# Channel mix in float32r over two-part coefficients, with contiguous row levels and whole column transforms

## The chip, the cores and the metric

The kernel runs on one core of one Trainium2 chip. The metric is the device time in microseconds of one execution, the median of the runs shown; a profile of one execution stands beside it. The engines are called PE (TensorE), DVE (VectorE), ACT (ScalarE), POOL (GpSimd) and SP (SyncE, which only issues transfers here).

## What is computed

The input x has the shape 4 x 64 x 256 x 256 (batch, channel, height, width), in float32. Four layers follow one another; 0, 1 and 3 are long convolutions, and layer 2 works in the Haar domain:

```python
# layers 0, 1, 3: a separable causal filter per channel, and a residual
k = einsum('ijk,imk->ijmk', hx, hy)[0]      # hx, hy: two small sine networks
y = irfft2(rfft2(x) * rfft2(k) / fft_size)[..., :L, :L]
x = y + x * bias[:, None, None]
# layer 2
f1 = haar2d(x)                               # rows and columns, 8 levels each
acc = 0
for i in range(2):
    f4 = einsum('bchw,oc->bohw', f1 * v[i], conv_w[i])
    acc = acc + sign(f4) * relu(abs(f4) - tau[i])
x = haar2d(acc, inverse=True) + x
```

## The kernel before

A convolution of layers 0, 1 and 3 is two products on PE with Toeplitz matrices, one for the columns and one for the rows; the Toeplitz tiles are read from short filters in device memory (pads) by overlapping rows. `contract` (L245) makes one such product as four matmuls in float32, two over 256 columns (L248) and two over 128 (L249).

`convolutions(b, ...)` takes one batch through layers 0 and 1 and the forward Haar transform, one channel at a time. `first` and `second` make the products a0, y0, a1, y1; ACT copies a0 and a1 from PSUM (L262), DVE adds the residual to y0 and y1 (L279). `pairs` (L312) makes the sums and differences of neighbouring columns into the tile `sd` (eight channels deep), `store` (L318) writes them to `keep` in device memory, for the end of layer 2. `levels` (L321) makes the other seven levels of the row transform for four channels at a time, in place in `sd`, with strides that double (L327 and L328, fourteen DVE instructions, of 512, 256, 128, 64, 32, 16 and 8 elements a partition, two each). The column transform inside a half of the rows is one product with a fixed matrix: `split` (L334, ACT) and `rest` (L339, DVE) cut a channel into two parts in the format float32r, and `down` (L344) adds two float32r products over 512 columns with the matrix `hbr` (L349). `down` also has a path that makes one float32 product with `hbt` (L353), which no channel takes, since `in_parts` is all channels. `away` (L358, ACT) copies the result from PSUM and SP writes it to `coef`.

`mixing(b, ...)` goes over 64 groups of four coefficient rows. `load` (L395) reads a group's coefficients of all 64 channels, two halves stacked on 128 partitions, from `coef` (SP, 3 buffers under the tag "f"). `mix` (L410) makes four float32 products a group, each with a slice of the coefficients as weights and a matrix `wb` as moving operand, 256 columns wide, which holds the mixing matrix twice with zeros between (L415). `scaled` (L432, DVE) and `scaled_too` (L436, ACT, one row of 64 elements an instruction, L439) multiply by v, then ACT takes the size and sign, DVE shrinks by tau and adds into `z`, which holds a whole batch in SBUF.

`inverse(b, ...)` takes z back, one channel at a time: `fetch` (L482) reads the kept sums and differences, `rows` (L491) makes the inverse row transform by products and transposes (L495, L496), `halves` (L501) splits the result into two float32r parts, `cols` (L507) makes the column product over 512 columns (L511), `join` (L516) adds the kept part and undoes `pairs`, and layer 3 follows. For batches 0 to 2 every third channel's layer 3 is put off: its u goes to `late` in device memory, and `convolution` (L545) takes it up beside the last mixing.

The order of the work is written out by hand. Each step is put into a list with a time in ticks (`at`, L296): the tick of its channel or group plus a fixed offset in `PLACE`. The list is sorted by this time, and the instructions are issued in that order; each engine takes its own in that order. Mixing of batch b runs beside the convolutions of batch b+1, whose 64 channels `spread` (L559) lays over the ticks up to the mixing's end; then the inverse of batch b follows with the rest of those convolutions. `border` is the tick at which a mixing ends; steps of a batch's last two groups of channels that are due after it are set three times as far apart (`after`, L304).

Of the kernel before, what the change touches and what calls it, by code (L numbers as in the profile page):

```python
# [41 lines left out]
    "away": 0.734,  # L42
    "mix load": -0.977,
# [52 lines left out]
def conv_seq_kernel(ctx, tc, x, fz, fw, bias, decay, haar, haar_row, factors, vt, taut, wmix, out):  # L96
# [33 lines left out]
    wb = const.tile([P, 2, P], F32, name="wb")  # L130
# [5 lines left out]
    sd = zpool.tile([P, 8, 2, 2, P], F32, name="sd")  # L136
    keep = [dram.tile([C, P, 2, 2, P], F32, name=f"keep{b}") for b in range(B)]
    coef = [dram.tile([2, C, P, S], F32, name=f"coef{b}") for b in range(B)]
# [67 lines left out]
    def constants():  # L206
        signs = part(P)
        nc.sync.dma_start(hbt, haar[0])
        nc.sync.dma_start(signs, haar[1])
        nc.sync.dma_start(hrow, haar_row)  # L210
        nc.vector.memset(wb, 0.0)
        for r in range(2):
            nc.sync.dma_start(wb[r * C : (r + 1) * C, r, :], wmix)
        nc.scalar.copy(hb, signs)
        nc.scalar.copy(hbr, hbt)
# [83 lines left out]
    def convolutions(b, ticks, in_parts=(), border=None):  # L299


        st = {}

# [8 lines left out]
        def pairs(c):  # L312
            v = st.pop(c)["y1"].rearrange("p k (w e) -> p k w e", e=2)
            t = sd[:, c % 8]
            nc.vector.tensor_add(t[:, :, 0, :], v[:, :, :, 0], v[:, :, :, 1])
            nc.vector.tensor_sub(t[:, :, 1, :], v[:, :, :, 0], v[:, :, :, 1])

        def store(c):  # L318
            nc.sync.dma_start(keep[b][c], sd[:, c % 8])

        def levels(steps):  # L321
            def run(n):
                t = sd[:, n % 2 * 4 : n % 2 * 4 + 4]
                for step in steps:
                    v = t[:, :, :, 0, :].rearrange("p c k (w e) -> p (c k) w e", e=2 * step)
                    even, odd = v[:, :, :, 0], v[:, :, :, step]
                    nc.vector.tensor_sub(odd, even, odd)  # L327
                    nc.vector.scalar_tensor_tensor(even, even, 2.0, odd, ALU.mult, ALU.subtract)  # L328

            return run  # L330

        parts = {}

        def split(c):  # L334

            w = parts[c] = mx.tile([P, 2, 2, S], F32R, name=f"sp_{b}_{c}", tag="sp", bufs=1)
            nc.scalar.copy(w[:, 0], sd[:, c % 8].rearrange("p k e w -> p k (e w)"))  # L337

        def rest(c):  # L339
            w = parts[c]  # L340
            t = sd[:, c % 8].rearrange("p k e w -> p k (e w)")
            nc.vector.tensor_tensor(w[:, 1], t, w[:, 0].bitcast(F32), ALU.subtract)  # L342

        def down(c):  # L344
# [7 lines left out]
            else:  # L352
                nc.tensor.matmul(  # L353
                    ps.rearrange(flat), hbt, sd[:, c % 8].rearrange("p k e w -> p (k e w)"), start=True, stop=True
# [3 lines left out]
        def away(c):  # L358
            t = io.tile([P, 2, S], F32, name=f"co_{b}_{c}", tag="co", bufs=BUFS["co"])
            nc.scalar.copy(t, parts.pop(("ps", c)))  # L360
            nc.sync.dma_start(coef[b][:, c].rearrange("k p w -> p k w"), t)
# [16 lines left out]
        for n in range(C // 4):  # L378
            end = ticks[4 * n + 3] + 4
            for s, steps in enumerate([(1,), (2, 4), (8, 16, 32, 64)]):  # L380
                at(after(end + 1 + s, n) + PLACE["levels"], levels(steps), n)
            for j in range(4):
                c = 4 * n + j
                if c in in_parts:
# [3 lines left out]
                at(after(end + 4 + j, n) + PLACE["away"], away, c)  # L388
        return after(ticks[-1] + 11, C // 4 - 1)

    def mixing(b, start, n_act):
# [3 lines left out]
        def load(g):  # L395
            f = mx.tile([P, 2, S], F32, name=f"f_{b}_{g}", tag="f", bufs=3)
            nc.sync.dma_start(f, coef[b].rearrange("k c p w -> (k c) p w")[:, 2 * g : 2 * g + 2])
# [12 lines left out]
        def mix(g):  # L410
            f = st[g]["f"]
            ps = psx.tile([P, 2, 2, S], F32, name=f"px_{b}_{g}", tag="mix")
            for q in range(2):
                for h in range(2):
                    nc.tensor.matmul(  # L415
                        ps[:, h, q, :],
                        f[:, q, h * P : (h + 1) * P],
                        wb.rearrange("p r n -> p (r n)"),
                        start=True,
                        stop=True,  # L420
                    )
# [288 lines left out]
```

## Time and profile before

| | |
|---|---|
| median of 3 runs | 2973.84 us (2973.59 to 2974.6) |
| span of the profiled execution | 2971.0 us; no other time is listed for it |
| PE busy | 2905.9 us (98%) |
| DVE busy | 2529.6 us (85%) |
| ACT busy | 2183.4 us (73%) |
| POOL busy | 0.2 us |
| transfers | 649.74 MB, mean 219 GB/s |

The span runs from the first to the last instruction of one execution. An engine is busy while one of its instructions lasts; matmul lengths are modelled and overlap, so their starts say more than their lengths. PEld is the loading of weights, which can lie beside a product. A row of a group of instructions has the line, the engine, the operation, what it writes and reads, its size and count, then the busy time in us and the mean of one in ns, then the idle time of the engine ahead of it and what ended that. A float32 product appears as two records, a float32r product as one. The columns of a table by stage are: the stage, its length, then busy time and count of PE, PEld, DVE, ACT and POOL, the clock, the busy share of the transfer engines, and GB/s.

### The profile page before, as it was taken

The page shows a single profiled execution, that of the slowest core. Times are in us where ns is not written, and L with a number is a line of the kernel's source. Part 1 is how long each engine was busy: PE and PEld are TensorE (multiplying, and loading weights), DVE is VectorE, ACT ScalarE, POOL GpSimd, SP SyncE. Part 2 cuts the span into 40 slices and gives each one's busy share as a digit, 9 for nine tenths or more (in the row PEclk, how much of TensorE's full clock was granted, in tenths as well). Part 3 has the DMA queues.
Part 4 walks back from the last instruction along what each step waited for, and adds up shares of the span by engine and source line. Part 5 has one row for each costly group of instructions (what it writes and reads, how often), then busy time and mean ns, then how long its engine had stood idle before and what let it go on. Part 6 is the DMA issues. An engine that isn't in the chain of part 4 may idle for free. (4 is left out here: it accounts for less than half of the span.)

```text
span 2971.0 us, 52173 instructions
## 1 busy us (share of the span) xinstructions
PE 2905.9 (98%) x16950; PEld 2615.2 (88%) x16950; DVE 2529.6 (85%) x4571; ACT 2183.4 (73%) x5142; POOL 0.2 (0%) x4
## 2 busy tenths in 40 slices
PE   8999999999999999999999999999999999999999
PEld 6899988888888998888888998888888998888998
DVE  5766768999988879999988878999998889998776
ACT  2333338999986768889986768999986768887554
POOL 0000000000000000000000000000000000000000
PEclk9999999999999999999999999999999999999999
DMA  5887777776667876767777876777677888777676
GB/s 156 246 235 230 225 234 213 210 208 195 210 196 238 255 222 199 210 209 208 209 220 229 255 228 199 210 211 211 206 211 231 255 245 235 234 231 220 212 211 186
DMA packets 562498, 649.74 MB, mean 219 GB/s; under 512 B 44369, under 2 KB 447412, under 8 KB 562100
## 3 DMA queue, kind: packets, MB, share of 16 engines
q1 hardware_dynamic: 482996, 562.07, 64.8%
q10 hardware_dynamic: 79232, 84.34, 8.1%
q8 instruction: 137, 2.24, 0.3%
q14 instruction: 133, 1.09, 0.1%
HBM read 426.77 MB, written 219.48 MB: 218 GB/s over the span
## 5 line engine op out<-in xcount | busy, mean ns | idle before, releaser
L248 PE MATMUL py<-t,a 128*128 128x256 f32 x3072 | 920.4, 381 | 11.7 <-ACT a L262 6.3
L262 ACT COPY a<-pa 128x512 f32<-128x512 f32 x768 | 485.8, 633 | 374.7 <-PE pa L249 338.9
L439 ACT ACTIVATE f<-px,vt 128x64 f32<-128x64 f32 x2816 | 619.9, 391 | 113.8 <-DVE f L434 113.2
L249 PEld LDWEIGHTS py<-t,a 128*128 128x128 f32 x3072 | 583.4, 190 | 79.4
L249 PE MATMUL py<-t,a 128*128 128x128 f32 x3072 | 590.0, 274 | 0.0
L248 PEld LDWEIGHTS py<-t,a 128*128 128x128 f32 x3072 | 498.4, 191 | 57.4 <-ACT a L262 18.1
L415 PE MATMUL px<-wb,f 128*128 128x256 f32 x2048 | 486.6, 380 | 6.4 <-ACT f L439 6.4
L415 PEld LDWEIGHTS px<-wb,f 128*128 128x128 f32 x2048 | 369.2, 190 | 48.3 <-ACT f L439 8.5
L248 PE MATMUL pa<-t,y 128*128 128x256 f32 x1024 | 310.0, 385 | 16.7 <-DVE y L279 15.4
L450 DVE TENSOR_TENSOR mag<-mag,vt 128x1024 f32<-128x1024 f32 x256 | 313.3, 1224 | 10.8 <-ACT mag L443 10.2
L443 ACT ACTIVATE mag<-f 128x1024 f32<-128x1024 f32 x256 | 299.8, 1171 | 20.4 <-DVE z L458 19.6
L454 DVE SCALAR_TENSOR_TENSOR mag<-mag,f 128x1024 f32<-128x1024 f32 x256 | 313.3, 1224 | 0.9
L504 ACT CAST w<-pw 128x512 fp32r<-128x512 f32 x256 | 150.3, 587 | 221.6 <-PE pw L496 208.9
L248 PE MATMUL pa<-t,x 128*128 128x256 f32 x1024 | 305.8, 380 | 1.1 <-issue 1.1
L446 ACT ACTIVATE f<-f 128x1024 f32<-128x1024 f32 x256 | 288.1, 1125 | 4.4 <-DVE y L279 1.2
L488 ACT COPY zc<-z 128x512 f32<-128x512 f32 x256 | 282.5, 1104 | 10.9 <-DVE z L289 6.3
L342 DVE TENSOR_TENSOR sp<-sd,sp 128x512 fp32r<-128x512 f32 x256 | 176.5, 689 | 105.0 <-ACT sp L337 103.6
L248 PE MATMUL pa<-t,u 128*128 128x256 f32 x772 | 231.0, 381 | 10.2 <-issue 9.5
L519 DVE SCALAR_TENSOR_TENSOR t<-r,pu 128x512 f32<-128x512 f32 x256 | 175.5, 685 | 65.6 <-PE pu L511 65.0
L279 DVE SCALAR_TENSOR_TENSOR y<-x,bsb,py 128x512 f32<-128x512 f32 x256 | 190.8, 745 | 39.3 <-PE py L249 39.2
L279 DVE SCALAR_TENSOR_TENSOR y<-y,bsb,py 128x512 f32<-128x512 f32 x256 | 190.3, 744 | 38.0 <-PE py L249 37.8
L249 PEld LDWEIGHTS pa<-t,y 128*128 128x128 f32 x1024 | 194.5, 190 | 26.4
(67 smaller groups left out, 4470.8 us busy)
## 6 DMA issues: line engine op xcount, KB each, us to landing
t<-pad SPq DMA_DIRECT2D x768, 256.0 KB, 3.9
x<-in_x SPq DMA_DIRECT2D x256, 256.0 KB, 3.6
keep<-sd SPq DMA_DIRECT2D x256, 256.0 KB, 2.9
coef<-co SPq DMA_DIRECT2D x256, 256.0 KB, 3.1
f<-coef SPq DMA_DIRECT2D x256, 256.0 KB, 3.3
r<-keep SPq DMA_DIRECT2D x256, 256.0 KB, 3.3
out_y<-y ACTq DMA_DIRECT2D x256, 256.0 KB, 4.0
late<-u ACTq DMA_DIRECT2D x63, 256.0 KB, 3.0
```

The source lines that it names most:

```text
L248: nc.tensor.matmul(ps[:, m, :], src[:, 0, m * P : (m + 1) * P], t[:, ::-1], start=True, stop=False)
L249: nc.tensor.matmul(ps[:, m, P:], src[:, 1, m * P : (m + 1) * P], t[:, : P - 1 : -1], start=False, stop=True)
L262: nc.scalar.copy(a, s["p" + new])
L279: nc.vector.scalar_tensor_tensor(y, s[res], bsb[:, layer, c : c + 1], s["p" + new], ALU.mult, ALU.add)
L342: nc.vector.tensor_tensor(w[:, 1], t, w[:, 0].bitcast(F32), ALU.subtract)
L415: nc.tensor.matmul(ps[:, h, q, :], f[:, q, h * P : (h + 1) * P], wb.rearrange("p r n -> p (r n)"), start=True, stop=True,)
L439: nc.scalar.mul(f4[:, j], px[:, j], scale(g, 0)[:, j : j + 1])
L443: nc.scalar.activation(mag, st[g]["f4"], AF.Abs)
L446: nc.scalar.activation(st[g]["f4"], st[g]["f4"], AF.Sign)
L450: nc.vector.tensor_sub(mag, mag, over(g, 1, 16))
L454: nc.vector.scalar_tensor_tensor(mag, mag, 0.0, st[g]["f4"], ALU.max, ALU.mult)
L488: nc.scalar.copy(a, z[:, :, :, c].rearrange("p h (i k) -> p h k i", k=2))
```

## The change

- The coefficients are stored in two float32r parts, high and low: `away` casts to float32r on ACT and writes the high part, a new step `low` (offset 1.05) subtracts it from PSUM on DVE and writes the rest. `coef` doubles in size; each part of a channel is written in rows of 2 KB a partition.
- `wb` holds the mixing matrix in two float32r parts. `mix` makes 16 float32r products a group, of 128 columns each: for every slice of 128 coefficient columns, one with the low and one with the high part of the matrix. High and low coefficients of the 64 channels are stacked on the 128 partitions. The group's load is 512 KB, is issued from POOL, and has 2 buffers.
- The kept sums and differences are written by two transfers, and `fetch` takes its tile from the buffers of x (tag "in").
- The row levels read and write contiguous halves, through `sums` and `less`; those of 128 and 64 stay on DVE, those of 32 to 2 are on POOL.
- `in_parts` is now filled inside `convolutions`: a channel is split only for batch 0 or where its column transform is due at or after the mixing's end; the others take the float32 product of `down`.
- Layouts of `sd`, of the inverse's tiles and of the host's tables follow; the space that POOL's transfers reserve is set to 1024.

```diff
-    wb = const.tile([P, 2, P], F32, name="wb")
+    wb = const.tile([P, 2, P], F32R, name="wb")
+    sums = zpool.tile([P, 4, 2, P], F32, name="sums")
+    less = zpool.tile([P, 4, 2, 96], F32, name="less")
-    coef = [dram.tile([2, C, P, S], F32, name=f"coef{b}") for b in range(B)]
+    coef = [dram.tile([2, C, P, 2, S], F32, name=f"coef{b}") for b in range(B)]
...
+            nc.vector.tensor_add(sums[:, c % 4], v[:, :, :, 0], v[:, :, :, 1])
+            nc.vector.tensor_sub(sd[:, c % 8, 1], v[:, :, :, 0], v[:, :, :, 1])
...
-            nc.sync.dma_start(keep[b][c], sd[:, c % 8])
+            nc.sync.dma_start(keep[b][c, :, 0], sums[:, c % 4])
+            nc.sync.dma_start(keep[b][c, :, 1], sd[:, c % 8, 1])
+        def levels(engine, lengths):
             def run(n):
-                t = sd[:, n % 2 * 4 : n % 2 * 4 + 4]
-                for step in steps:
-                    v = t[:, :, :, 0, :].rearrange("p c k (w e) -> p (c k) w e", e=2 * step)
-                    even, odd = v[:, :, :, 0], v[:, :, :, step]
-                    nc.vector.tensor_sub(odd, even, odd)
-                    nc.vector.scalar_tensor_tensor(even, even, 2.0, odd, ALU.mult, ALU.subtract)
+                t = sd[:, n % 2 * 4 : n % 2 * 4 + 4, 0]
+                for length in lengths:
+                    half = length // 2
+                    v = place(t, length).rearrange("p c k (w e) -> p c k w e", e=2)
+                    engine.tensor_tensor(place(t, half), v[..., 0], v[..., 1], ALU.add)
+                    engine.tensor_tensor(t[:, :, :, half:length], v[..., 0], v[..., 1], ALU.subtract)
+        def place(t, length):
+            if length == P:
+                return sums
+            if length == 1:
+                return t[:, :, :, :1]
+            begin = {64: 0, 32: 64, 16: 0, 8: 16, 4: 24, 2: 28}[length]
+            return less[:, :, :, begin : begin + length]
...
-            t = io.tile([P, 2, S], F32, name=f"co_{b}_{c}", tag="co", bufs=BUFS["co"])
-            nc.scalar.copy(t, parts.pop(("ps", c)))
-            nc.sync.dma_start(coef[b][:, c].rearrange("k p w -> p k w"), t)
+            t = parts["hi", c] = mx.tile([P, 2, S], F32R, name=f"hi_{b}_{c}", tag="hi")
+            nc.scalar.copy(t, parts["ps", c])
+            nc.sync.dma_start(coef[b][0, c].rearrange("p k w -> p (k w)"), t.bitcast(F32).rearrange("p k w -> p (k w)"))
+        def low(c):
+            t = mx.tile([P, 2, S], F32R, name=f"lo_{b}_{c}", tag="lo", bufs=1)
+            nc.vector.tensor_tensor(t, parts.pop(("ps", c)), parts.pop(("hi", c)).bitcast(F32), ALU.subtract)
+            nc.sync.dma_start(coef[b][1, c].rearrange("p k w -> p (k w)"), t.bitcast(F32).rearrange("p k w -> p (k w)"))
...
-            for s, steps in enumerate([(1,), (2, 4), (8, 16, 32, 64)]):
-                at(after(end + 1 + s, n) + PLACE["levels"], levels(steps), n)
+            at(after(end, n) + PLACE["levels"], levels(nc.vector, (128,)), n)
+            at(after(end + 1, n) + PLACE["levels"], levels(nc.vector, (64,)), n)
+            at(after(end + 1, n) + PLACE["levels"], levels(nc.gpsimd, (32, 16, 8, 4, 2)), n)
             for j in range(4):
                 c = 4 * n + j
-                if c in in_parts:
+                if border is None or end + 4 + j >= border:
+                    in_parts.add(c)
...
+                at(after(end + 4 + j, n) + PLACE["low"], low, c)
...
-            f = mx.tile([P, 2, S], F32, name=f"f_{b}_{g}", tag="f", bufs=3)
-            nc.sync.dma_start(f, coef[b].rearrange("k c p w -> (k c) p w")[:, 2 * g : 2 * g + 2])
+            f = mx.tile([P, 2, 2, S], F32R, name=f"f_{b}_{g}", tag="f", bufs=2)
+            nc.gpsimd.dma_start(f, coef[b].rearrange("l c p k w -> (l c) p k w")[:, 2 * g : 2 * g + 2])
...
-            for q in range(2):
-                for h in range(2):
-                    nc.tensor.matmul(
-                        ps[:, h, q, :],
-                        f[:, q, h * P : (h + 1) * P],
-                        wb.rearrange("p r n -> p (r n)"),
-                        start=True,
-                        stop=True,
-                    )
+            for h in range(2):
+                for q in range(2):
+                    for r in range(2):
+                        for i in (1, 0):
+                            nc.tensor.matmul(
+                                ps[:, h, q, r * P : (r + 1) * P],
+                                f[:, q, h, r * P : (r + 1) * P],
+                                wb[:, i],
+                                start=(i == 1),
+                                stop=(i == 0),
+                            )
...
-            r = mx.tile([P, 2, 2, P], F32, name=f"r_{b}_{c}", tag="f", bufs=3)
+            r = io.tile([P, 2, 2, P], F32, name=f"r_{b}_{c}", tag="in", bufs=3)
...
-    ready = convolutions(0, range(C), in_parts=range(C))
+    ready = convolutions(0, range(C))
...
-            ready = convolutions(b + 1, spread(ahead, end + 2), in_parts=range(C), border=end)
+            ready = convolutions(b + 1, spread(ahead, end + 2), border=end)
...
-    nc = _bacc.Bacc("TRN2", target_bir_lowering=False, num_devices=1)
+    nc = _bacc.Bacc("TRN2", target_bir_lowering=False, num_devices=1, dynamic_dma_scratch_size=1024)
```

## The prediction

> **What bounds the kernel now.** I read the page's first two parts, then each stage by windows of time, then the timeline of TensorE, because an engine that looks 98% busy may only be waiting between instructions.
>
> ```profile
> span 2971.0 us, 52173 instructions
> PE 2905.9 (98%) x16950; PEld 2615.2 (88%) x16950; DVE 2529.6 (85%) x4571; ACT 2183.4 (73%) x5142; POOL 0.2 (0%) x4
> ```
>
> Busy time per engine in the four mixing stages (from the first to the last product of L415):
>
> ```profile
> 453.00:858.00 405.00, 398.49 (x2179) 350.37 (x2179) 381.86 (x671) 396.73 (x1203) 0.00 (x0) 1.00 0.69 205
> 1088.00:1529.00 441.00, 435.14 (x2440) 391.42 (x2440) 409.39 (x717) 388.21 (x1094) 0.00 (x0) 1.00 0.71 208
> 1763.00:2203.00 440.00, 434.70 (x2436) 390.99 (x2435) 408.86 (x717) 387.70 (x1093) 0.00 (x0) 1.00 0.70 208
> 2433.00:2705.00 272.00, 266.62 (x1450) 238.83 (x1450) 265.13 (x313) 234.87 (x555) 0.00 (x0) 1.00 0.80 234
> ```
>
> TensorE idles 6 us in each of them, 23 us in all; DVE and ACT are at 88 to 98%, so they are close behind. The timeline of TensorE tells whether its busy time is real work; columns are start, length, line, records in a row:
>
> ```profile
> 1502.95 1.89 PE L415 MATMUL px<-wb,f 128*128 128x256 f32 x8
> 1504.68 0.59 PE L248 MATMUL py<-t,a 128*128 128x256 f32 x2
> 1505.11 0.38 PE L249 MATMUL py<-t,a 128*128 128x128 f32 x2
> 1505.33 0.60 PE L248 MATMUL py<-t,a 128*128 128x256 f32 x2
> ...
> 1507.08 0.38 PE L249 MATMUL pa<-t,x 128*128 128x128 f32 x2
> 1507.22 0.71 PE L349 MATMUL pz<-sp,hbr 128*128 128x512 f32 x2
> 1507.77 0.59 PE L248 MATMUL py<-t,a 128*128 128x256 f32 x2
> ```
>
> Starts, not lengths, give the cost, since lengths overlap. A float32 product is two records. The 8 records of one mixing group take 1504.68 - 1502.95 = 1.73 us (0.216 each, 256 columns); two of 128 columns take 1505.33 - 1505.11 = 0.22 us (0.11 each): the cost goes with the columns. The two float32r products of 512 columns begin after the pair at 1507.08 (0.22 us) and end at 1507.77: 0.47 us, 0.235 each. With these prices TensorE's work is 8192 x 0.216 (L248, L415) + 6144 x 0.11 (L249) + 1536 x 0.11 (L495, L496) + 1024 x 0.235 (L349, L511) = 2855 us of 2971. **The kernel is bound by TensorE's own work**, and any added product shows in the time.
>
> One more thing decides this case: what a weight load costs when no product hides it. At 113.9 us TensorE had been idle:
>
> ```profile
> 113.92 0.30 PEld L349 LDWEIGHTS pz<-sp,hbr 128*128 128x128 f32 x2 [0.80 <-issue]
> 114.26 0.19 PEld L248 LDWEIGHTS py<-t,a 128*128 128x128 f32 x1
> ```
>
> A load lasts 0.19 in the records, so the second of the pair began at 113.92 + 0.30 - 0.19 = 114.03, 0.11 us after the first. In the dense stretches each load begins as the product before it begins; so the first float32r product could start only 0.11 us after its load. The two products use the same weights (hbr) and are still loaded twice: L349 has 512 products and 512 loads.
>
> **What the Trainium skill says.** "FP8 and Floating Point Precision", TensorE Precision Notes: true FP32 takes four passes. The trace agrees: 256 columns take 2 x 0.216 us, and float32r 512 columns take 0.235 instead of four times as much. "TensorE: Matmul & The Clock Gate", LDWEIGHTS (loading the stationary operand): a load takes columns / 1.2 ns, 107 ns for 128; the trace's 0.11 agrees. The same page, Weight-path perf modes, says that the fast weight load is off for FP32 input; the 0.11 is float32r's, so it has none either. "SBUF — State Buffer", Who interferes with whom: a DVE instruction with two SBUF inputs and a GpSimd instruction that reads SBUF block each other; GpSimd does nothing in this trace, so no run here shows it.
>
> **The change part by part.**
> *Channel mix (L415).* It removes 8 records of 0.216 (1.73 us) per group and adds 16 float32r products of 128 columns, each with its own weight load, since both coefficient parts times both weight parts are summed. The trace has no float32r product of 128 columns. By its columns one takes 128/512 of 0.235 = 0.06, or 0.075 if the 0.02 that 0.235 has above 512 columns' 0.213 (twice 256 columns' single pass, 0.107) is fixed. But its load takes 0.11 and begins only as the product before starts, so 0.11 is the pace: 16 x 0.11 = 1.76 us, +0.03 us, **+8 us** for 256 groups. Bounds: 0.06 each (-197 us) and the float32 price, 0.22 (+458 us). I take 0.11, because a load is seen in the trace for every product.
> *Whole column transforms (down).* Their transforms for batches 1 to 3 that come due before the mixing's end are made in float32 in one product, without split and rest. From the ticks of spread(): 54, 53 and 53 channels; the other 10, 11 and 11 and all 64 of batch 0 stay in parts. One costs 4 passes of 512 columns = 4 x 0.216 = 0.86 us instead of 0.47: 160 x 0.39 = **+62 us**, on the bound engine. Removed beside it: 160 times ACT's split and DVE's rest, 115 and 110 us.
>
> ```profile
> L337 ACT CAST sp<-sd 128x512 fp32r<-128x512 f32 x256 | 184.0, 719 | 3.9 <-DVE sd L328 3.9
> L342 DVE TENSOR_TENSOR sp<-sd,sp 128x512 fp32r<-128x512 f32 x256 | 176.5, 689 | 105.0 <-ACT sp L337 103.6
> L505 DVE TENSOR_TENSOR w<-pw,w 128x512 fp32r<-128x512 f32 x256 | 175.3, 685 | 2.3 <-ACT w L504 2.3
> L327 DVE TENSOR_TENSOR sd<-sd 128x512 f32<-128x512 f32 x64 | 44.2, 691 | 47.9 <-DMA keep<-sd 28.2 <-DMA t<-pad 12.0 <-DMA coef<-co 2.5
> ```
>
> *low.* 256 DVE subtractions from PSUM, priced as L505: +175 us of DVE. Each waits for ACT's copy (away) and holds the bank pz about 0.3 tick longer; the fourth bank after it is wanted 0.6 tick later still, so TensorE doesn't wait. Its store waits on SP behind DVE; queued behind it are keep, x and t loads that have about a tick (6.5 us) of lead.
> *Row levels.* They are 64 x 5.15 us = 330 us on DVE (L327 and L328). Two of 512 at 0.69 and two of 256 at 0.42 (L315's price) remain, 143 us. Ten GpSimd instructions a group take the rest: 496 elements at the 4497 ns for 2048 of the page "GPSIMD Engine Reference", 3.1 Elementwise, are an estimated 1.1 us, and 0 to 0.5 us each fixed: 1 to 6 us of a group's 26. They may hold DVE as long. In the second mixing stage DVE had 409 us; with low (57 x 0.69), less levels (57 x 0.73) and rest (53 x 0.69), it has 370, and with 14 groups at 6 us 454 of some 463. So TensorE's work hides it at both ends, narrowly at the upper; past that, each us of DVE is a us of time.
> *Transfers.* coef is written and read in two parts: 2 x 256 x 256 KB = 134 MB more than 649.74. In a mixing stage that is 441 us x 208 GB/s = 92 MB plus 64 x 0.26 + 57 x 0.26 = 32 MB, so 0.71 of the engines becomes about 0.91 in a stage 22 us longer. The f loads move from SP past POOL's level instructions, with 2 buffers for 3: a load may start when the product two groups before is done, two ticks less 1.76 us before its use, 11 us (6.7 in the last mixing stage). The price from "DMA: Bandwidth & Descriptors", Anatomy of one DMA, 2.0 us + 524288/436000 = 3.2 us alone, fits; doubled by traffic it still fits, so nothing on the path, bound 0 to +64 us. SP gains 512 issues (second keep, second coef) and loses 256, at 0.33 us: 85 us of an engine that mostly waits. r moves into the buffers of x; both are live two ticks, so in the three or so ticks where a new batch's loads meet an inverse stage 4 are wanted of 3: about +3 us at each of three such places, **+9 us**. The relief of ACT and DVE may give back a third of the 23 us of idle: **-7 us**.
> Sum: 8 + 62 + 9 - 7 = **+72 us**. On the profiled span, 2971 + 72 = 3043; the median shown lies 2.8 us above this span, so 3046.
>
> **The rivals.**
> *A slower pace:* float32r in 128 columns goes at the float32 price, 0.22. For it: only 512 columns have been seen. Against it: float32 halves exactly with its columns. 2974 + 458 + 62 + 2 = 3496 us.
> *The load doesn't bind* (the side that ends faster): the loads of successive small products overlap and the pace is 0.075: 16 x 0.075 = 1.20, -0.53 us a group, -136 us; with 62 and -7, 2893 us. It decides from 1.73 - 62/256 = 1.49 us a group, 0.093 us a product. Against it: the 0.11 at 113.92.
> *Transfers bind:* at 0.91 the tiles f, x or t land late. 0.25 us a group is +64 us: 3110 us. For it: the doubled traffic and POOL's queue; against it: TensorE hardly waits at 0.80 in the last mixing stage.
>
> **How the numbers follow.** Load-bound pace 0.68, own range 3025 to 3080; transfers 0.12; slower pace 0.16; faster 0.04. The range 3015 to 3130 holds the first two, with the unknown GpSimd and transfer costs. A difference of 0.2% (6 us) is about what a measurement can tell from no change: slower 0.95, the same 0.01, faster 0.04.
>
> **What would show it.** The mix's 16 products 0.11 us apart, 1.76 us a group, with PEld near 100% there; about 160 float32 products of 512 columns, two records 0.43 apart; ACT and DVE near 80% in the mixing stages while TensorE stays at 98%. It is wrong if the 16 take 1.5 us or 3.5 us, or if TensorE waits for f.

## The result, and the profile after

The changed kernel takes 3418.53 us (median of 4 runs, 3414.4 to 3419.87) against 2974.22 us before (4 runs): 1.149 times as long, with a 95% interval of 1.147 to 1.151. The forecast was 3046 us with a range up to 3130. The direction was right, and the added time is 444 us instead of 72. The profiled execution has a span of 3418.1 us.

The first line of the page after and its line of busy times:

```profile
span 3418.1 us, 57457 instructions
PE 3123.2 (91%) x18998; PEld 2783.1 (81%) x18998; DVE 2453.4 (72%) x4027; ACT 2111.5 (62%) x4983; POOL 343.8 (10%) x900
```

No engine is as busy as the busiest was before: TensorE fell from 98% to 91%, DVE from 85 to 72%, ACT from 73 to 62%. So the question is which engine waits for which. The same four stages as before (first to last product of the mix, now L439); the columns are the stage, its length, busy time and count of PE, PEld, DVE, ACT and POOL, the clock, the transfers' share and GB/s:

```profile
457.00:987.00 530.00, 460.16 (x2686) 397.76 (x2685) 359.24 (x550) 381.58 (x1154) 79.80 (x192) 0.93 0.69 212
1217.00:1771.00 554.00, 499.11 (x2982) 437.34 (x2980) 384.96 (x595) 364.30 (x1049) 80.44 (x202) 0.96 0.74 219
2001.00:2555.00 554.00, 491.83 (x2976) 429.67 (x2974) 384.04 (x594) 363.41 (x1048) 80.48 (x202) 0.97 0.73 219
2786.00:3148.00 362.00, 302.28 (x1969) 279.12 (x1969) 278.37 (x318) 241.44 (x562) 32.82 (x62) 0.93 0.76 221
```

They have grown from 405, 441, 440 and 272 us by 125, 113, 114 and 90: 442 us, all that was lost. Between and around the stages nothing moved by more than 5 us. Inside them TensorE now stands idle for 55 to 70 us each, where it was about 6 before. DVE and ACT have less work than before in the first three and a little more in the fourth, and are busy only 66 to 77% of the time.

Was TensorE's new work mispriced? Its timeline says no (start, length, line, records in a row):

```profile
1303.60 0.38 PE L253 MATMUL py<-t,a 128*128 128x128 f32 x2
...
1304.48 0.60 PE L252 MATMUL pa<-t,y 128*128 128x256 f32 x2
1304.91 0.38 PE L253 MATMUL pa<-t,y 128*128 128x128 f32 x2
1305.05 1.98 PE L439 MATMUL px<-wb,f 128*128 128x128 f32 x16
1306.87 0.65 PE L252 MATMUL py<-t,a 128*128 128x256 f32 x2
1307.35 0.38 PE L253 MATMUL py<-t,a 128*128 128x128 f32 x2
1307.57 0.60 PE L252 MATMUL py<-t,a 128*128 128x256 f32 x2
...
1309.54 1.02 PE L367 MATMUL pz<-sd,hbt 128*128 128x512 f32 x2
```

From the first of the 16 products to the next instruction it is 1306.87 - 1305.05 = 1.82 us. But the first one's record begins 0.14 us after a pair that takes 0.22 elsewhere, and the pair behind takes 0.48 in place of 0.43. The price of a group is seen better from the pair ahead to the end of the second pair behind, 1307.57 - 1304.91 = 2.66 us, less the same three pairs without a group, 1304.48 - 1303.60 = 0.88: 1.78 us. The median over such places is 1.79 us, or 16 times the 0.112 us from one product to the next; 1.76 was forecast. Counted alike, the group took 1.73 before. There are 320 records of L367, 160 whole transforms, as counted. TensorE's work grew by about what the prediction said. The waits of the whole run tell where the rest went (who waited, for whom, us in total, times, longest):

```profile
ACT f L463 <- DVE f L458: 623.0, 252, 8.6
DVE mag L474 <- ACT mag L467: 378.6, 185, 3.4
DVE lo L379 <- ACT hi L374: 247.9, 159, 3.5
PE py L252 <- ACT a L266: 130.5, 91, 3.2
PE pa L252 <- DVE y L283: 96.9, 84, 3.6
```

Before, the first of these (then ACT at L439 for DVE at L434) was 113.2 us in 131 waits, and the second (DVE at L450 for ACT at L443) 10.2 us in 31. ACT waits for `scaled`, DVE for `size`: the steps of one group wait for one another. TensorE, in the last two lines, waits for ACT's copies a and DVE's sums y of the convolutions (6.3 us in 11 waits and 15.4 in 22 before): these stand in the same two queues, behind the steps of the mixing. One tick of the mixing, DVE first and then ACT:

```profile
1301.05 0.42 DVE L458 TENSOR_TENSOR f<-px,vt 128x256 f32<-128x256 f32 x1
1301.38 0.74 DVE L283 SCALAR_TENSOR_TENSOR y<-x,bsb,py 128x512 f32<-128x512 f32 x1
1305.54 1.23 DVE L474 TENSOR_TENSOR mag<-mag,vt 128x1024 f32<-128x1024 f32 x1 [3.42 <-ACT mag L467]
1306.68 0.69 DVE L379 TENSOR_TENSOR lo<-pz,hi 128x512 fp32r<-128x512 f32 x1
1307.28 0.74 DVE L283 SCALAR_TENSOR_TENSOR y<-y,bsb,py 128x512 f32<-128x512 f32 x1
1307.94 1.22 DVE L478 SCALAR_TENSOR_TENSOR mag<-mag,f 128x1024 f32<-128x1024 f32 x1
...
1309.74 0.69 DVE L482 TENSOR_TENSOR z<-mag 128x512 f32<-128x512 f32 x1
1310.35 0.42 DVE L458 TENSOR_TENSOR f<-px,vt 128x256 f32<-128x256 f32 x1
```

```profile
1301.50 2.57 ACT L463 ACTIVATE f<-px,vt 128x64 f32<-128x64 f32 x12 [2.35 <-DVE f L458]
1303.88 0.67 ACT L266 COPY a<-pa 128x512 f32<-128x512 f32 x1
1304.35 1.16 ACT L467 ACTIVATE mag<-f 128x1024 f32<-128x1024 f32 x1
...
1310.80 1.55 ACT L463 ACTIVATE f<-px,vt 128x64 f32<-128x64 f32 x7 [3.38 <-DVE f L458]
```

Read the steps of one group: `scaled` (L458) at 1301.05, `scaled_too` (L463) 1301.50, `size` (L467) 1304.35, `shrink` (L474) 1305.54, `signed` (L478) 1307.94, `add` (L482) 1309.74, and only then, at 1310.35, `scaled` of the next group. This tick lasts 9.3 us, and in it ACT idles while DVE has the group and DVE idles (3.42 us) while ACT has it. The kernel before did the same steps in another order:

```profile
1303.01 1.22 DVE L450 TENSOR_TENSOR mag<-mag,vt 128x1024 f32<-128x1024 f32 x1
1304.14 0.42 DVE L434 TENSOR_TENSOR f<-px,vt 128x256 f32<-128x256 f32 x1
1304.48 1.22 DVE L454 SCALAR_TENSOR_TENSOR mag<-mag,f 128x1024 f32<-128x1024 f32 x1
...
1306.27 0.69 DVE L458 TENSOR_TENSOR z<-mag 128x512 f32<-128x512 f32 x1
```

Here `scaled` (L434) of the next group comes between `shrink` (L450) and `signed` (L454) of this one, so ACT starts on the next group while DVE finishes this one.

These lines also correct a sentence ahead of the prediction, that each engine takes its instructions in the order of the times in `PLACE`. By those times `scaled` of g+1 (g + 1.583) stands ahead of `shrink` of g (g + 1.777); in the lines above, of the kernel before, it comes after it. The framework that makes each engine's list of instructions from the program rearranges the order.

### The profile page after: what moved, and what is told of

The parts are those of the page before. It is cut to its first block, busy times and chain, and to the rows that moved or that the text cites. A ratio compares the mean times of both kernels' runs of the same rounds, so it can differ in the third digit from the quotient of the medians.

```text
span 3418.1 us, 57457 instructions
## 1 busy us (share of the span) xinstructions
PE 3123.2 (91%) x18998; PEld 2783.1 (81%) x18998; DVE 2453.4 (72%) x4027; ACT 2111.5 (62%) x4983; POOL 343.8 (10%) x900
## 5 line engine op out<-in xcount | busy, mean ns | idle before, releaser
L252 PE MATMUL py<-t,a 128*128 128x256 f32 x3072 | 962.9, 396 | 130.8 <-ACT a L266 130.5
L463 ACT ACTIVATE f<-px,vt 128x64 f32<-128x64 f32 x2816 | 609.4, 346 | 627.0 <-DVE f L458 623.0
L252 PEld LDWEIGHTS py<-t,a 128*128 128x128 f32 x3072 | 497.0, 196 | 222.5 <-ACT a L266 152.0
L253 PEld LDWEIGHTS py<-t,a 128*128 128x128 f32 x3072 | 601.5, 196 | 86.8
L253 PE MATMUL py<-t,a 128*128 128x128 f32 x3072 | 606.2, 280 | 0.0
L474 DVE TENSOR_TENSOR mag<-mag,vt 128x1024 f32<-128x1024 f32 x256 | 313.4, 1224 | 380.7 <-ACT mag L467 378.6
L439 PE MATMUL px<-wb,f 128*128 128x128 f32 x4096 | 527.7, 283 | 3.7 <-DVE z L482 2.1
L439 PEld LDWEIGHTS px<-wb,f 128*128 128x128 f32 x4096 | 498.1, 198 | 5.1 <-ACT f L463 4.5
L379 DVE TENSOR_TENSOR lo<-pz,hi 128x512 fp32r<-128x512 f32 x256 | 176.5, 689 | 276.8 <-ACT hi L374 247.9
L252 PE MATMUL pa<-t,x 128*128 128x256 f32 x1024 | 328.7, 404 | 29.2 <-DVE lo L379 19.7
L419 POOL DMA_DIRECT2D f<-coef x256 | 137.7, 538 | 1924.5 <-PE px L439 1576.0
L478 DVE SCALAR_TENSOR_TENSOR mag<-mag,f 128x1024 f32<-128x1024 f32 x256 | 313.1, 1223 | 15.1 <-ACT f L470 11.2
L467 ACT ACTIVATE mag<-f 128x1024 f32<-128x1024 f32 x256 | 291.5, 1139 | 1.7
L252 PEld LDWEIGHTS pa<-t,y 128*128 128x128 f32 x1024 | 157.3, 193 | 137.6 <-DVE y L283 129.6
L253 PEld LDWEIGHTS pa<-t,x 128*128 128x128 f32 x1024 | 204.0, 199 | 30.9
```

The source lines that it names most:

```text
L252: nc.tensor.matmul(ps[:, m, :], src[:, 0, m * P : (m + 1) * P], t[:, ::-1], start=True, stop=False)
L253: nc.tensor.matmul(ps[:, m, P:], src[:, 1, m * P : (m + 1) * P], t[:, : P - 1 : -1], start=False, stop=True)
L379: nc.vector.tensor_tensor(t, parts.pop(("ps", c)), parts.pop(("hi", c)).bitcast(F32), ALU.subtract)
L439: nc.tensor.matmul(ps[:, h, q, r * P : (r + 1) * P], f[:, q, h, r * P : (r + 1) * P], wb[:, i], start=(i == 1), stop=(i == 0),)
L463: nc.scalar.mul(f4[:, j], px[:, j], scale(g, 0)[:, j : j + 1])
L467: nc.scalar.activation(mag, st[g]["f4"], AF.Abs)
```

## The experiments

**Theory.** The mix part makes the framework issue another order on DVE and ACT, one group at a time in place of two under way, and that chain sets the mixing stages. **Rivals:** the new coupling of `low` to `hi`; GpSimd's instructions or the doubled transfers; slower products. For each run the table counts from its trace, over the 252 groups that have a next one in their batch, how many of the `shrink`, `signed` and `add` come on DVE ahead of the next group's `scaled` (252 of all three: never two groups under way).

| kernel | time, us | shrink / signed / add ahead | mixing stages, us |
|---|---|---|---|
| before | 2974 | 133 / 11 / 2 | 405, 441, 440, 272 |
| after | 3418.5 | 252 / 204 / 140 | 530, 554, 555, 361 |
| e1_pin2 | 3089.7 | 0 / 0 / 0 | 438, 472, 472, 296 |
| e2_b_collapse | 3226.1 | 194 / 190 / 189 | 535, 513, 513, 272 |
| e3_b_cols | 3050.5 | 163 / 115 / 2 | 425, 466, 466, 272 |
| e4_mix_only | 3401.6 | 249 / 173 / 90 | 519, 554, 552, 361 |
| e9_oldmix | 3019.8 | 168 / 96 / 2 | 414, 465, 465, 272 |
| e11_mix8 | 3054.6 | 155 / 94 / 2 | 419, 467, 466, 277 |
| e12_three_free | 2978.2 | 60 / 8 / 2 | 413, 438, 437, 278 |
| e13_four256 | 3009.1 | 125 / 13 / 2 | 413, 452, 452, 282 |
| e14_four128 | 3398.3 | 249 / 179 / 100 | 510, 554, 555, 362 |

**e1_pin2: force the order in the changed kernel.** The edge added fixes the order of issue of two instructions on DVE, with no wait.

```diff
+            begun[g] = nc.vector.tensor_tensor(st[g]["f4"][:, :n], px[:, :n], over(g, 0, n), ALU.mult)
...
-            nc.vector.tensor_sub(mag, mag, over(g, 1, 16))
+            later = nc.vector.tensor_sub(mag, mag, over(g, 1, 16))
+            if g + 1 in begun:
+                tc.add_manual_dep(
+                    later.ins,
+                    begun[g + 1].ins.name,
+                    mybir.DependencyInfo(mybir.DependencyClass.NoSync, mybir.DependencyReason.DATA),
+                    reason="order",
+                )
```

> The changed kernel with nothing but an order added: DVE's shrink of group g is issued after scaled of group g+1, so two groups are always under way, as they were before the change. Theory A (the order of the mixing steps on DVE and ACT collapsed to one group at a time, and that chain sets the mixing stages): the four mixing stages shrink from 531, 553, 555, 361 us to about 430, 465, 465, 290 us, and the time falls from 3418 to between 3040 and 3100 us. Rival B (the new coupling of low on DVE to hi on ACT stalls both): low still waits for hi and the time stays above 3300 us. Rival C (GpSimd's levels or the doubled transfers hold DVE or PE up): all of that is still there, so 3350 us or more. Rival D (the float32r products themselves are slower than 0.11 us): 3400 us or more.

Measured: 3089.71 us, 1.0385 times before (1.037 to 1.0401). Nothing but the order was changed, and 329 of the 444 us are back. TensorE is busy again for 463 of the second stage's 472 us:

```profile
1121.00:1593.00 472.00, 462.86 (x2980) 412.81 (x2978) 388.60 (x594) 364.86 (x1047) 102.80 (x200) 1.00 0.85 257
```

**e2_b_collapse: force the other order in the kernel before.** `PLACE` has shrink, signed and add at 1.577 to 1.579, and

```diff
+            if g - 1 in added:
+                tc.add_manual_dep(
+                    begun.ins,
+                    added[g - 1].ins.name,
+                    mybir.DependencyInfo(mybir.DependencyClass.NoSync, mybir.DependencyReason.DATA),
+                    reason="order",
+                )
...
```

> The kernel before with nothing but its order changed: in batches 0 to 2 shrink, signed and add of group g are issued before scaled of group g+1 on DVE, so one group is under way at a time; batch 3 is left alone. No float32r mixing, no low, no GpSimd, no more transfers. Theory A: the first three mixing stages grow as in the changed kernel or more, by 100 to 160 us each, so the time goes from 2974 to between 3270 and 3460 us; the fourth stage stays at 272 us. Rivals B, C and D: the order alone costs little, since none of their causes is there: 2974 to 3030 us.

Measured: 3226.11 us, 1.0845 (1.0829 to 1.0862). The order alone, with none of the change, costs 252 us: 130, 72 and 73 in the three stages touched, nothing in the fourth, and 23 less between the stages. That rules out the rivals as the main cause. The lower end expected, 3270, was missed by 44 us; the chain here has no `low` in it and lighter products, which may be why (not tried).

**e3_b_cols: the whole columns alone in the kernel before.**

```diff
-                if c in in_parts:
+                if border is None or end + 4 + j >= border:
+                    in_parts.add(c)
...
```

> The kernel before with the whole column transforms alone: 160 channels take one float32 product of 512 columns (two records of 0.43 us) in place of two float32r products of 0.235. Theory A and the sum of the prediction: +62 us for 160 x 0.39 us on TensorE, less some us of idle: 3020 to 3040 us; the mix steps stay interleaved by the add (add comes after the next scaled), though signed loses that in 117 of 192 groups, so up to 40 us more where that matters. Rival (the whole columns are a large part of the 445 us): above 3150 us.

Measured: 3050.49 us, 1.0255 (1.024 to 1.027): +76 us. The three stages with whole columns grew by 20, 25 and 26 us, each close to 53 x 0.39 = 21; the order changed too (`signed` comes early in 115 groups, for 11 before) while `add` stayed behind the next `scaled`; the 5 us a stage beyond 21 leave little room for that to have cost much.

**e4_mix_only: the mix part nearly alone.** The changed kernel with all levels on DVE and all columns in parts:

```diff
-            at(after(end + 1, n) + PLACE["levels"], levels(nc.gpsimd, (32, 16, 8, 4, 2)), n)
+            at(after(end + 1, n) + PLACE["levels"], levels(nc.vector, (32, 16, 8, 4, 2)), n)
...
-                if border is None or end + 4 + j >= border:
+                if True:
```

> The changed kernel with all row levels on DVE instead of GpSimd and every channel's column transform in two parts as before the change; what is left of the change is the two-part coefficients, the 16 float32r products, contiguous levels and two stores of keep. Theory A: the order is collapsed here as in the changed kernel, so the mixing stages stay at about 530 to 560 us, longer with rest, split and the levels in the loop: 3400 to 3550 us. Rival C by GpSimd (its instructions hold DVE): the mixing stages recover, below 3200 us. Rival B (low waits for hi): as theory A, 3400 us or more.

Measured: 3401.57 us, 1.1436 (1.1417 to 1.1455). Without GpSimd's levels and the whole columns the time is only 17 us lower, and the collapse is still there: it comes with the mix part.

**e5_pin2_nocols: e1 with all columns in parts** (the second edit of e4 alone).

> The first experiment's kernel (the changed kernel with two groups kept under way) with every channel's column transform in two float32r parts again. If the whole columns cost the same 76 us here as alone in the kernel before (160 channels, 0.39 us of TensorE each by the prediction, 62 us), the time falls from 3090 to between 3010 and 3030 us. Rival: rest and split come back to DVE and ACT (about 110 us each) and, with two groups under way and low added, DVE becomes the bound of the mixing stages: then less than 30 us is gained, 3060 us or more.

Measured: 3076.45 us, 1.034 (1.0313 to 1.0367). Only 13 us come back, not 76, as the rival expected. In its second stage TensorE is down to 445 of 461 us while DVE has 418:

```profile
1128.00:1589.00 461.00, 444.96 (x2986) 413.52 (x2985) 417.90 (x644) 391.17 (x1097) 105.66 (x201) 1.00 0.86 263
```

DVE, at 91%, is close behind TensorE and not alone the bound; over the run TensorE's waits for y grow from 22.0 us in e1 to 43.3, those for a from 6.1 to 15.5. What the whole columns add to TensorE they take from DVE and ACT, and with `low` in the loop that relief is worth most of its price.

**e6_before_pin2: the edge of e1 in the kernel before.**

> A control: the kernel before with the same order edge as the first experiment (shrink of g after scaled of g+1). If the edge only restores what the kernel before already has, it changes little: 2965 to 2985 us. If the edge is itself a better order than the kernel before's, some of the first experiment's 329 us would be a gain of the edge and not the loss undone: below 2960 us.

Measured: 2967.33 us, 0.9978 (0.9968 to 0.9988). The edge is worth 7 us there, so of the 329 us nearly all is a loss undone.

**e7_pin2_sp: e1 with f loaded from SP.**

```diff
-            nc.gpsimd.dma_start(f, coef[b].rearrange("l c p k w -> (l c) p k w")[:, 2 * g : 2 * g + 2])
+            nc.sync.dma_start(f.bitcast(F32), coef[b].rearrange("l c p k w -> (l c) p k w")[:, 2 * g : 2 * g + 2])
```

> The first experiment's kernel with the loads of f issued from SP instead of POOL, still with 2 buffers. In the first experiment TensorE waited 21 us for f, behind POOL's level instructions or behind the transfers. If POOL's queue makes f late, 15 to 25 us come back: 3065 to 3080 us. If the transfers or the two buffers make it late, nothing does: 3085 to 3095 us.

Measured: 3061.52 us, 1.0293 (1.0278 to 1.0309): 28 us come back, most in the first stage (438 to 419) and some in the last (296 to 290). First e1, then e7: TensorE's idle time ahead of the mix, and what ended it.

```profile
L440 PE MATMUL px<-wb,f 128*128 128x128 f32 x4096 | 513.9, 279 | 23.8 <-DMA f<-coef 21.2 <-DVE y L283 1.4 <-ACT a L266 0.8
```

```profile
L440 PE MATMUL px<-wb,f 128*128 128x128 f32 x4096 | 510.7, 278 | 9.5 <-DMA f<-coef 7.7 <-DVE mag L475 1.5 <-ACT f L471 0.2
```

A load from POOL landed 5.5 us after its issue, one from SP 4.7. In the last stage POOL has no level instructions, so these are not the whole reason; how the 28 us divide between POOL's queue and the slower landing stays open.

**e8_three: twelve products of 256 columns.** It leaves out low times low; the order of e1 and the loads of e7 are kept, the columns are in parts. The products themselves (the layout of coefficients and of `wb` follows):

```diff
+            for h in range(2):
+                for q in range(2):
+                    for n, (l, i) in enumerate(((0, 1), (1, 0), (0, 0))):
+                        nc.tensor.matmul(
+                            ps[:, h, q, :],
+                            f[:, l, q, h * P : (h + 1) * P],
+                            wb[:, i].rearrange("p r n -> p (r n)"),
+                            start=(n == 0),
+                            stop=(n == 2),
+                        )
...
```

> A version meant to beat both: order kept, column transforms in parts, row levels as in the changed kernel, and the mix as 12 float32r products a group over 256 columns (the wide matrix with zeros, rows of both halves stacked on the partitions as in the kernel before) in place of 16 over 128: high times low, low times high, high times high; it leaves out low times low. f is loaded from SP. If a product costs the larger of its load (0.11 us) and its columns (0.235/2 = 0.118 us), a group takes 12 x 0.118 = 1.42 us against 1.73 before, 80 us less over 256 groups: 2974 - 80 = 2894 us if TensorE stays the bound, up to 2940 with waits for ACT and DVE. If the pace of 0.11 were a cost of the small products and not of the load, 256 columns would take 0.22: 12 x 0.22 = 2.64 us a group, 2974 + 233 = 3207 us.

Measured: 2957.55 us, 0.9943 (0.9928 to 0.9957). The products of 256 columns start 0.120 us apart against 0.112 for 128 columns, so the pace of a product of 128 columns isn't set by its columns. Its load, 0.11 us from one to the next in the trace before, fits; as every product here has its own load, another fixed price of a product isn't ruled out. A group costs 1.44 us, counted as above from pair to pair, close to the 1.42 expected. But only the two middle stages gain (441 and 440 to 428 and 430); the first stays at 405 us, with DVE at 94% and ACT at 97% of it.

**e9_oldmix: all of the change but the mix.**

> The changed kernel with the mixing of the kernel before: four float32 products a group, coefficients in one part, no low, f loaded from SP with 3 buffers. Whole columns, contiguous levels with the small ones on GpSimd, two stores of keep and r in the buffers of x stay. Theory A (the mix part alone upsets the order): the steps stay interleaved and the time is that of the whole columns alone, 3050 us, within 20 us. Rival C (GpSimd's levels hold DVE, or r in the buffers of x holds the loads): above 3100 us.

Measured: 3019.81 us, 1.0149 (1.0134 to 1.0164). Two groups stay under way in part (no `add` moves ahead, but 96 `signed` do), and it is 30 us better than expected, for which the next run has the reason.

**e10_levels: the row levels in the kernel before**, with what hangs on them in the change: the two stores of keep, and r in the buffers of x.

> The kernel before with the row levels alone: contiguous halves, those of 128 and 64 on DVE, those of 32 to 2 on GpSimd, keep stored by two transfers; columns in two parts and the float32 mix as before. The prediction let these cost nothing and DVE fall by 187 us in all (330 to 143): between 2960 and 2976 us, since TensorE has only 23 us of idle in the mixing stages. Rival: GpSimd's instructions hold DVE as long as they run, some 4 us of a group's 26, and the later end of the levels makes the column transforms late: 2985 us or more.

Measured: 2950.95 us, 0.9915 (0.9901 to 0.993), a gain of 25 us. The mixing stages have kept their lengths (403, 440, 440, 273): the gain lies in the parts between them, 230, 234 and 230 us before and 221, 226 and 226 here, and ahead of the first.

**e11_mix8: eight of the sixteen products.**

```diff
-                        for i in (1, 0):
+                        for i in (0,):
...
-                                start=(i == 1),
+                                start=True,
```

> The changed kernel with 8 of the 16 products of a group: those with the low part of the mixing matrix are left out, so the output is computed with the matrix's high part alone. low, hi, f on POOL, GpSimd's levels and the whole columns stay, no order is forced. TensorE's work falls by 256 x 8 x 0.112 = 229 us. Theory A in the form that the count of products upsets the order: with 8 the steps stay interleaved (add of g after scaled of g+1), and the time is 3090 - 229 = 2861 us if TensorE stays the bound, up to 2960 us where DVE and ACT are it. If low or the transfers upset the order or are themselves the cost, the chain of one group stays and only TensorE's part of it, 0.9 us of a 9.3 us tick, goes: 3200 us or more.

Measured: 3054.59 us, 1.0263 (1.0246 to 1.028), between the two expectations. `add` is back behind the next `scaled`, so `low` and the transfers don't upset the order; but `signed` is still ahead of it in 94 groups, about as in e9 (96), which has the old mix, so that part of the order goes with the whole columns and not with the products; and TensorE is busy for only 429 of the second stage's 467 us, with 123 us of DVE waiting for `size` over the run and 165 us for `hi`. It was wrong to count this as the old order: the steps overlap in part.

**e12_three_free: e8 without the forced order.**

> The version with 12 products over 256 columns without the forced order. If 12 products leave the order interleaved, the edge is not needed: 2950 to 2975 us. If the two-part coefficients upset it whatever the products are, the mixing stages grow by 70 to 130 us each: 3200 us or more.

Measured: 2978.19 us, 1.0008 (1.0 to 1.0017). No collapse: `add` stays behind the next `scaled` in all but 2 groups. The edge is worth 21 us here.

**e13_four256 and e14_four128: the count of products, or their form?** Both have 16 products a group, columns in parts, f from SP, no forced order. e13 is e12 with low times low put back; e14 is the changed kernel with the columns of e5 and the loads of e7.

> The version with 256-column products of the twelfth experiment, with the fourth part-product (low times low) put back: 16 float32r products a group, as many as in the changed kernel, but of 256 columns; no order forced. TensorE has 256 x 4 x 0.12 = 123 us more than with 12. If the count of 16 upsets the order, one group at a time: 3250 us or more. If the 128-column form does, the order stays interleaved here: 2978 + 123 = 3101 us, down to 3060 where TensorE's new work lies in its waits.

> The partner of the run before: the changed kernel's 16 float32r products of 128 columns a group, with the columns in parts and f loaded from SP as there; no order forced. If the 128-column form upsets the order: 3250 us or more, mixing stages of 500 us and more. If it takes something else of the changed kernel (the whole columns, f on POOL): 3050 to 3110 us.

Measured: 3009.06 us, 1.012 (1.0105 to 1.0135), and 3398.26 us, 1.1426 (1.1409 to 1.1443). The same sums in as many products, 389 us apart. The second stage of each, e13 and then e14:

```profile
1099.00:1551.00 452.00, 450.58 (x2980) 421.42 (x2980) 411.80 (x641) 387.51 (x1097) 70.61 (x132) 1.00 0.88 268
```

```profile
1196.00:1750.00 554.00, 483.69 (x2978) 441.31 (x2978) 417.60 (x644) 390.80 (x1097) 61.43 (x140) 0.94 0.71 219
```

TensorE, DVE and ACT have nearly the same work; ACT's wait for `scaled` is 128 us over the run in e13 and 514 in e14. So neither the count alone nor the two-part coefficients upset the order, but sixteen products in the 128-column form. Eight of them don't. e13 also lays the coefficients out otherwise, and its copies write them in another pattern; e11 keeps the changed kernel's layout and copies and still doesn't collapse, so these alone are not the cause. Nor is TensorE's real time: a group costs it 1.92 us in e13 and 1.79 in the changed kernel. What the framework weighs when it orders them no trace shows; that it takes a 128-column product for longer than the 0.112 us measured would fit, and is only argued.

**e15_levels_pin: the two edits that gained, in the kernel before.**

> The kernel before with the row levels of the change (25 us faster alone) and the order edge (7 us faster alone). If the two gains are of different places (levels outside the mixing stages, the edge inside), they add up: 2940 to 2947 us. If both are the same relief of DVE, 2948 to 2952 us.

Measured: 2943.18 us, 0.99 (0.9883 to 0.9916). They add up, and this beats both kernels. Its busy times, beside the kernel before's 2905.9 us of TensorE and 2529.6 of DVE:

```profile
span 2941.2 us, 52915 instructions
...
PE 2894.8 (98%) x16950; PEld 2615.1 (89%) x16950; DVE 2395.6 (81%) x3931; ACT 2181.9 (74%) x5142; POOL 322.5 (11%) x644
```

## Why the prediction was wrong

Put one after the other, the runs divide the 444 us so: row levels with r and the two stores -25 (e10), the whole columns +69 (e9 less e10), the mix part with two groups under way +70 (e1 less e9), its order +329 (after less e1). The parts depend on one another, as e5 shows, so this is one way to lay them out. With the order restored the time comes near the forecast of 3046: 3090 in e1, inside the forecast range of 3015 to 3130, and 3062 with f from SP (e7). That is partly luck: the row levels gained more than forecast, the mix part cost more.

**The step that failed** is the one that priced all work off TensorE at nothing on the path: "So TensorE's work hides it at both ends", and likewise "so TensorE doesn't wait". It compared sums of busy time, DVE's 370 to 454 us against a stage of 463, and took the order of the steps as given. The sum was right: DVE has 385 us in the second stage. But a busy share below 100% hides nothing when the order puts DVE's and ACT's shares end to end, as in the tick above: ACT waited 623 us for `scaled` in place of 113, TensorE waited 227 us for a and y in place of 22, and the order was worth 329 us. No step priced the order, and no rival named it. The line that could have warned was in the trace before: ACT waited 113 us for `scaled`, while TensorE's share left no slack for a longer tick.

*What bounds it, and the pace.* Right for the kernel before, and for the pace. The 16 products cost 1.79 us (1.76 forecast), 0.06 more than before: +15 us instead of +8. The load's price of 107 ns by the Trainium skill, "TensorE: Matmul & The Clock Gate", LDWEIGHTS, agrees with the 0.112 between starts, and e8 shows that twice the columns cost only 0.008 more. One reading isn't in the records: the product whose load begins at 113.92 begins at 113.95, not 0.11 us after it; the pace needs only that the two loads are 0.11 apart. The rivals of a slower pace (0.22) and of a faster one (0.075) are both out; that the first's 3496 us is near the result is chance.

*Whole columns.* Right in mechanism: 160 x 0.39 = 62 forecast, 76 measured alone. The step had no room for the relief of DVE to matter; with `low` in the loop it gives back most of it (e5).

*low.* Its size was right (0.69 us each). TensorE did wait for it, 24 us in the changed kernel, where the whole loop waits; with the order restored (e1) it is 2.5 us. Of the mix part's 70 us the products account for 15 and f from POOL for 28 (e7); how much of the rest is `low` is not shown.

*Row levels.* The gain was undersized: -25 us in e10, where -7 was forecast for all relief, and most of it lies outside the mixing stages. GpSimd's ten instructions hold DVE up only a little (last section).

*Transfers.* Half right: with the order restored they reach 0.83 to 0.91 of the engines (0.91 was forecast), and f's price of "nothing on the path, bound 0 to +64" was 28 us from POOL (e7). In the changed kernel as it is, the longer stages leave them at 0.69 to 0.76, so the rival by transfers decided nothing there.

*r in the buffers of x.* +9 us was forecast; no run parts it from the row levels, and e10, which has both, is 25 us faster than the kernel before.

*What would show it.* The signs named for the pace came as forecast, so did the 160 whole transforms (records of L367 0.43 us apart), and "ACT and DVE near 80% in the mixing stages while TensorE stays at 98%" did not: that sentence held the test of the failed step.

## What to carry to other kernels

When a change alters the instructions of a pipelined loop, its order on the engines that share the loop is part of the change: before pricing sums of busy time, write down which step of which item comes between which on each engine, and price the loop if one item had to finish before the next begins. If all engines fall well below their limits at once, look for two engines that wait for each other, and test by forcing the order before touching the work. Bundled edits should be tried one by one: here the row levels gained 25 us, and the order edge 7 in the kernel before, beside a change that lost 444.

## What the runs showed of the hardware

A TensorE that waits also becomes slower. In the changed kernel, after an idle stretch of 2.15 us, the same pair of products takes 0.86 us from start to start (at 1292.26) where it took 0.43 (at 1291.45); from 1291.92 to 1295.33 the trace has a granted clock of 0.50:

```profile
1290.69 0.70 PE L252 MATMUL py<-t,a 128*128 128x256 f32 x2 [2.15 <-ACT a L266]
1291.23 0.38 PE L253 MATMUL py<-t,a 128*128 128x128 f32 x2
1291.45 0.60 PE L252 MATMUL py<-t,a 128*128 128x256 f32 x2
1291.88 0.59 PE L253 MATMUL py<-t,a 128*128 128x128 f32 x2
1292.26 1.06 PE L252 MATMUL pa<-t,x 128*128 128x256 f32 x2
1293.12 0.63 PE L253 MATMUL pa<-t,x 128*128 128x128 f32 x2
...
1295.94 0.59 PE L252 MATMUL pa<-t,y 128*128 128x256 f32 x2
```

The Trainium skill, "TensorE: Matmul & The Clock Gate", Part 1: The HAM clock gate, describes windows of 3.4 us at half the clock after idleness. The trace agrees in the half and in the length. The page asks for a whole idle window of about 3.4 us first; here 2.15 us were enough, and in the 3.4 us ahead of the slow stretch TensorE had been busy for 37%. The changed kernel has 46 such slow stretches, of 3.4 us or two or three times that, and the kernel before has none; this is why the mixing stages after show a granted clock of 0.93 to 0.97 where those before show 1.00. The new products are not the cause: e2, which has none of them, shows 0.93 in its first stage. So a wait of TensorE can cost more than its own length.

GpSimd's and DVE's instructions hold each other up. In e10 a GpSimd addition of 16 elements a partition, 0.21 us elsewhere, lasts as long as the `shrink` beside it:

```profile
1368.82 0.23 POOL L332 TENSOR_TENSOR sd<-less 128x32 f32<-128x32 f32 x1
1368.84 1.30 DVE L467 TENSOR_TENSOR mag<-mag,vt 128x1024 f32<-128x1024 f32 x1
1369.02 1.20 POOL L331 TENSOR_TENSOR less<-less 128x16 f32<-128x16 f32 x1
1370.17 0.40 POOL L332 TENSOR_TENSOR sd<-less 128x16 f32<-128x16 f32 x1
```

The other way round the price is smaller, since GpSimd's instructions are short. The `shrink` in these lines begins while a GpSimd instruction runs and lasts 1.30 us. In e10, 38 of the 256 `shrink` begin so, and they take 1283 ns on average; the other 218 take 1219. Over all 256 the mean is 1228, against 1224 in the kernel before without GpSimd, so the mean alone hides it. The prediction cited the Trainium skill, "SBUF — State Buffer", Who interferes with whom, for both blocking each other; the trace agrees for both sides.
